# Attention row sums of an adaLN transformer block: transposed and reduced on VectorE in blocks 3 to 14, with a lower threshold for clearing banks on ScalarE

## The chip, the core and the metric

The kernel runs on one core of a Trainium2 chip. The metric is device time in microseconds (us), the median over runs of the same program. The five engines of the core run their own instruction streams in order: TensorE (PE in the profile, its weight loads PEld), VectorE (DVE), ScalarE (ACT), GpSimd (POOL) and SyncE (SP, which issues nearly all transfers here).

## What is computed

One transformer block with adaptive layer norm on 8 sequences of 1024 rows and width 512. The rows are cut in halves of 512, so each sequence gives batches of T = 512, and attention runs over 16 heads of width 32. The reference, cut to what matters:

```python
mod = silu(condition) @ Wada + bada            # six rows of shifts, gains, gates
xm = layernorm(x, g1, be1) * (1 + sc_a) + sh_a
q, k, v = split_heads(xm @ Wqkv)               # 16 heads of width 32
scores = where(causal, q @ k.T * 32 ** -0.5, -inf)
attn = softmax(scores)                         # exp(..) / sum over the keys
x = x + gt_a * (merge_heads(attn @ v) @ Wproj + bproj)
xm = layernorm(x, g2, be2) * (1 + sc_m) + sh_m
x = x + gt_m * (gelu(xm @ W1 + b1) @ W2 + b2)
```

All of it is in float32; the causal mask runs over the full 1024 rows of a sequence. The change concerns the sum over the keys under the softmax, its reciprocal and the division.

## The kernel before, in words

**Blocks.** The work is tiled in 16 blocks n of 512 rows (8 sequences, each with a first half h = 0 and a second half h = 1; odd n are second halves, which look back on the keys of both halves). Each block has four groups g of four heads (HPG = 4; a head has hd = 32 columns, so a group fills the 128 partitions). The dense products (k, q, v, the two layers of the MLP) go through one level of Strassen's scheme with 256-column products; every product is four matmuls side by side, each for 32 of the 128 output partitions (`matmul`, the line 217 of the profile).

**Planner.** The program is built by a Python planner, not by hand. It keeps a clock for each engine (`now`), when each datum is written (`written`) and when its last reader is done (`left`), with estimated costs that `note`, `note_pe` and `note_act` add. A main thread walks through the dense steps of the blocks in the order of `plan`; side threads hold steps that wait for something. The attention (`attend`) is walked in order, and before each of its steps `step_aside` lets dense work go first if that is ready sooner. `stream["due"]` paces the two against each other. So the order of the instructions on each engine comes from the estimates; on the chip each engine simply runs its queue in order.

**Jobs.** Work on VectorE that is not urgent lies in a list (`add_job`); `run_jobs` emits a job when the planner's VectorE is not ahead of TensorE and the job's data are due, `run_jobs(True)` emits all of them at once. Jobs marked `first` go ahead of others.

**Banks.** Three PSUM banks (`banks`, tags l0 to l2) serve all dense products, the row maxima and the row sums. A thread that wants a bank names `BANK` among its needs. They are emptied by `copy_out` (lines 194 and 197, on VectorE or ScalarE, whichever the planner has free sooner) and by `combine_out`, which adds another term: on VectorE straight from the bank (line 208), or, where the planner's VectorE is more than 3500 ns behind its ScalarE, by a copy on ScalarE (line 204) and an addition afterwards on VectorE or GpSimd (`either`, lines 167 and 170). Four more banks hold one tile "st", in turn for scores (line 1595, reduced to maxima on VectorE by lines 1607 and 1610) and for the transposed scores (lines 1674 and 1686, which ScalarE turns into weights by exp, line 1698). One more bank, "po", holds the weighted values of a group (line 1726).

**Weights and slots.** The exponentials of one unit (up to four heads by 512 queries, for 128 keys) lie in a tile `pT` in one of three SBUF slots (`free_p`, tags p0 to p2). The first unit of a group becomes the accumulator `acc`; GpSimd adds the later units of the group onto it (`add_weights`, line 1816). At the end of a group, `finish` has TensorE sum `acc` over the 128 keys that are left: four matmuls by a tile of ones (line 1747), each over 512 columns, into one of the three banks; the result stands in all 32 partitions of its head. Then the slot is free again. ScalarE copies the sums to `rec` (line 1756) and the weighted values to `top` (line 1759); VectorE takes the reciprocals in four jobs of 128 columns (line 1765, `invert`); GpSimd multiplies `top` by `rec` into `qTs[n]` (line 1790, `quotient`), from which the projection `project_out` reads later. With 16 blocks of four groups there are 64 such ends.

Of the kernel before, what the change touches and what calls it, by code (L numbers as in the profile page):

```python
# [9 lines left out]
F32 = mybir.dt.float32  # L10
# [12 lines left out]
def kernel(  # L23
# [89 lines left out]
    def note(engine, ns, reads=(), writes=(), port=False):  # L113
        start = max(now[engine], due(reads, writes))
        if port:
            start = max([start] + [b for a, b in pool_spans if a <= start < b])
        end = start + ns
        now[engine] = end
        if engine == "POOL":
            pool_spans.append((start, end))  # L120
            del pool_spans[:-16]
        for k in reads:
            left[k] = max(left.get(k, 0.0), end + SYNC)
        for k in writes:
            written[k] = end + SYNC
        return end
# [9 lines left out]
    def note_pe(ns, form, reads=(), writes=()):  # L136
        now["PE"] = max(now["PE"], due(reads, writes))
        if shape[0] != form:
            shape[0] = form
            now["PE"] += SWITCH  # L140
        note("PE", ns, reads)
        spent[0] += ns
        for k in writes:
            written[k] = now["PE"] + PIPE

    def note_act(ns, func, reads=(), writes=()):
        if func is not None and table[0] != func:
            table[0] = func
            ns += TABLE
        note("ACT", ns, reads, writes)  # L150
# [49 lines left out]

    def combine_out(out, bank, src, other, reads=(), writes=(), op=ALU.add, last=True):
        ready = due([("l", bank)], writes)
        if op is ALU.add and out is not other and max(now["DVE"], ready) > max(now["ACT"], ready) + 3500:
            nc.scalar.copy(out, src)
            note_act(585, None, [("l", bank)], writes)
            either(out, out, other, op, [*reads, *writes], writes)
        else:
            nc.vector.tensor_tensor(out, src, other, op)  # L208
            note("DVE", 690, [("l", bank), *reads], writes)
        live[bank] = not last  # L210
# [214 lines left out]
    nc.gpsimd.memset(eps, EPS)  # L425
    ones = const.tile([P, hd], F32, tag="ones", name="ones")
    nc.gpsimd.memset(ones, 1.0)
    minus_half = const.tile([P, NTT], F32, tag="minus_half", name="minus_half")
    nc.gpsimd.memset(minus_half, -0.5)
    minus_ones = const.tile([P, P], BF16, tag="minus_ones", name="minus_ones")  # L430
# [122 lines left out]
    def add_job(job, reads, first=False):  # L553

        at = sum(1 for other in jobs if other[2]) if first else len(jobs)
        jobs.insert(at, (job, reads, first))

    def run_jobs(everything=False):
        while jobs and (
            everything or (now["DVE"] <= now["PE"] and due(jobs[0][1]) <= now["PE"])  # L560
        ):
            jobs.pop(0)[0]()
# [841 lines left out]
    def start(it):  # L1404
        thread = [it, None]
        sides.append(thread)
        advance(thread)
# [255 lines left out]
    def weights_T(n, g, parts):  # L1663

        h = blocks[n][1]
        qT = qTs[n]
        reads = [("qT", n), ("kT", n)] + [("mrow", n, gg) for gg in {part[3] for part in parts}]
        step_aside(reads, ["st"])
        st = ps_st.tile([P, HPG, TB], F32, tag="st", name=f"st_{n}_{g}_{parts[0][0]}")
        for k, c0, w, gg in parts:  # L1670
            row = m_rows[n, gg]
            for j in range(HPG):
                r = slice(j * hd, (j + 1) * hd)
                nc.tensor.matmul(  # L1674
                    st[:, j, c0 : c0 + w],
                    minus_ones[r, :],
                    row[r, TB - w :],
                    start=(c0 == 0),
                    stop=False,
                    skip_group_check=True,  # L1680
                )
        for k, c0, w, gg in parts:
            kT = keys_of(n, k // NTT)
            for j in range(HPG):
                r = slice(j * hd, (j + 1) * hd)
                nc.tensor.matmul(  # L1686
                    st[:, j, c0 : c0 + w],
                    kT[r, gg, ts(k % NTT, P)],
                    qT[r, gg, TB - w :],
                    start=False,  # L1690
                    stop=True,
                    skip_group_check=True,
                )
            note_pe(2.5 * COLUMN * w, "rows", reads, ["st"])
        slot = free_p.pop(0)
        pT = pp.tile([P, HPG, TB], F32, tag=f"p{slot}", name=f"pT_{n}_{g}_{parts[0][0]}")
        used = parts[-1][1] + parts[-1][2]
        nc.scalar.activation(pT[:, :, :used], st[:, :, :used], AF.Exp, scale=scale)  # L1698
        note_act(170 + 3.34 * used, "exp", ["st"], [("p", slot)])
        if parts[0][0] >= h * NTT:  # L1700
            for _, c0, _, _ in parts:
                diagonal = pT[:, :, c0 : c0 + P]
                nc.gpsimd.affine_select(  # L1703
                    diagonal,
                    diagonal,
                    pattern=[[0, HPG], [1, P]],
                    compare_op=ALU.is_ge,
                    fill=0.0,
                    base=0,
                    channel_multiplier=-1,  # L1710
                )
                note("POOL", 700, [("p", slot)], [("p", slot)])
        return pT, slot
# [22 lines left out]
    def finish(n, g):  # L1736

        run_jobs(True)
        acc, slot = totals.pop((n, g))
        more = unadded if (n, g) == first_end else []  # L1740
        step_aside([("acc", n, g), *(("p", slot) for *_, slot in more)], [BANK])
        bank = lin_bank()
        terms = [(0, TB, acc, slot)] + [(c0, w, pT, slot) for parts, pT, slot in more for _, c0, w, _ in parts]
        for i, (c0, w, term, held) in enumerate(terms):
            for j in range(HPG):
                r = slice(j * hd, (j + 1) * hd)
                nc.tensor.matmul(  # L1747
                    banks[bank][r, TB - w :], ones, term[:, j, c0 : c0 + w],
                    start=i == 0, stop=i == len(terms) - 1, skip_group_check=True,
                )  # L1750
            note_pe(2 * COLUMN * w, "columns", [("acc", n, g), ("p", held)], [("l", bank)])
        free_p.extend([slot, *(held for *_, held in more)])
        top = tmp.tile([P, TB], F32, tag="top", name=f"top_{n}_{g}", bufs=1)
        rec = tmp.tile([P, TB], F32, tag="rec", name=f"rec_{n}_{g}", bufs=1)
        kr = "rec"
        nc.scalar.copy(rec, banks[bank])  # L1756
        note_act(585, None, [("l", bank)], [kr])
        live[bank] = False
        nc.scalar.copy(top, outs.pop((n, g)))
        note_act(585, None, ["po"], ["top"])  # L1760
        part = TB // 4

        def invert(i):
            some = rec[:, i * part : (i + 1) * part]
            nc.vector.reciprocal(some, some)  # L1765
            note("DVE", 920, [kr], [kr])

        if (n, g) == groups[-1]:
            for i in range(NTT):
                invert(i)  # L1770
                some = slice(i * part, (i + 1) * part)
                nc.vector.tensor_tensor(qTs[n][:, g, some], top[:, some], rec[:, some], ALU.mult)
                note("DVE", 200, [kr, "top"], [("att", n, i)])
            return

        if (n, g) == first_end:
            for i in range(NTT):
                invert(i)
            nc.vector.tensor_tensor(qTs[n][:, g, :], top, rec, ALU.mult)
            note("DVE", 700, [kr, "top"], [("att", n)], port=True)  # L1780
            written["attended", n] = 0.0
            return

        def quotient():
            invert(3)
            if n == NB - 1 and g == NC - 2:
                nc.vector.tensor_tensor(qTs[n][:, g, :], top, rec, ALU.mult)
                note("DVE", 700, [kr, "top"], [("att", n)], port=True)
            else:
                nc.gpsimd.tensor_tensor(qTs[n][:, g, :], top, rec, ALU.mult)  # L1790
                note("POOL", 1285, [kr, "top"], [("att", n)])
            if g == NC - 1:
                written["attended", n] = 0.0

        for i in range(3):
            add_job(lambda i=i: invert(i), [kr], g == NC - 1)
        add_job(quotient, [kr], g == NC - 1)

    shared = {}

# [193 lines left out]
```

## Time and profile before

| | |
|---|---|
| median of 3 runs | 3505.04 us (3502.97 to 3507.28) |
| the profiled execution | 3510.74 us, its span 3509.0 us |
| granted TensorE clock | 0.998 |
| PE, matmuls | 3454.3 us busy |
| DVE | 2198.9 us |
| POOL | 2084.2 us |
| ACT | 1212.4 us |
| first and last row sums of blocks 3 to 14 | 645.5 and 3098.5 us from the span's start |

The profile's rows name a line of the kernel, an engine, the tiles written and read, and how often ("x512"). A float32 matmul is recorded as two instructions, so the four matmuls of one row sum are eight records ("x8"). The row of a timeline has the start, the length, the engine, and in brackets how long the engine had been idle and what ended that. In the view of waits a row has the engine and line that waited, what for, the sum in us, how often, and the longest. In the view of windows a row has the window, its length, and for each engine (in the order PE, PEld, DVE, ACT, POOL, as far as it occurs) the busy us with the count of instructions, then the granted clock, the share of the DMA engines and GB/s.

### The profile page before, as it was taken

How to read it: one execution, taken by the hardware profiler on the slowest of the kernel's cores; microseconds unless marked ns; L12 is line 12 of the kernel's file. 1: busy time of each engine (PE TensorE's matmuls, PEld its weight loads, DVE VectorE, ACT ScalarE, POOL GpSimd, SP SyncE). 2: the span in 40 equal slices, each digit the busy share in tenths (PEclk: the TensorE clock that was granted, in tenths of full speed). 3: DMA queues.
4: the chain of work that ended last, by engine and by line, in shares of the span. 5: the costliest groups of instructions: out<-in, count | busy, mean ns of one | idle time of the engine just before them, and what ended most of it. 6: DMA issues, size and time to landing. Idle time of an engine off the chain costs nothing.

```text
span 3509.0 us, 120365 instructions
## 1 busy us (share of the span) xinstructions
PE 3454.3 (98%) x54429; PEld 1724.0 (49%) x54429; DVE 2198.9 (63%) x2401; ACT 1212.4 (35%) x1276; POOL 2084.2 (59%) x2258
## 2 busy tenths in 40 slices
PE   8999999999999999999999999999999999999999
PEld 4444445445554545445454454544555444554445
DVE  5766676564666656665666566765666756656563
ACT  2335333342233423335223342333423343232531
POOL 3767846666366663756727576275753658537660
PEclk9999999999999999999999999999999999999999
DMA  6843444535545445363454534545354544443334
GB/s 212 263 137 104 137 115 140 142 107 159 142 125 156 119 147 153 119 170 115 137 157 130 155 117 144 150 137 148 116 155 137 165 122 146 128 136 101 96 121 140
DMA packets 328194, 491.10 MB, mean 140 GB/s; under 512 B 27260, under 2 KB 177596, under 8 KB 324100
## 3 DMA queue, kind: packets, MB, share of 16 engines
q1 hardware_dynamic: 327568, 483.39, 47.1%
q8 instruction: 428, 7.01, 0.8%
q14 instruction: 82, 0.67, 0.1%
q10 hardware_dynamic: 116, 0.03, 0.0%
HBM read 425.57 MB, written 55.64 MB: 137 GB/s over the span
## 4 chain that ended last, share of the span: by engine, by line
PE 83%; POOL 7%; DMA 3%; DVE 3%; ACT 1%; issue 1%; SPq 1%; ACTq 0%; DVEq 0%; POOLq 0%
PE bank L217 59%; PE sc L1595 8%; PE st L1686 6%; PE po L1726 6%; POOL pT L1816 4%; PE st L1674 2%; PE bank L1747 2%; DMA hat_m<-held_m 1%; DVE mx L1610 1%; POOL hT L170 1%; ACT pT L1698 1%; DMA held_m<-xm_m 1%; PE bank L1648 0%; POOL xr L170 0%; DMA w<-in_L_cond_Wqkv_dram 0%
## 5 line engine op out<-in xcount | busy, mean ns | idle before, releaser
L1816 POOL TENSOR_TENSOR pT<-pT,pT 128x256 f32<-128x256 f32 (+3 forms) x1254 | 1219.7, 1007 | 298.5 <-PE po L1726 181.6
L1698 ACT ACTIVATE pT<-st 128x2048 f32<-128x2048 f32 x288 | 540.9, 1878 | 1065.1 <-PE st L1686 959.8
L217 PE MATMUL bank<-w,hT 128*32 128x256 f32 x14336 | 823.7, 380 | 0.4 <-issue 0.4
L1610 DVE TENSOR_REDUCE mx<-sc 128x4 f32<-128x2048 f32 (+3 forms) x384 | 665.9, 1755 | 235.6 <-PE sc L1595 229.5
L217 PEld LDWEIGHTS bank<-w,hT 128*32 128x32 f32 x14336 | 446.7, 110 | 390.3 <-issue 105.8
L217 PE MATMUL bank<-xm_m,w 128*32 128x256 f32 x8192 | 498.6, 381 | 3.6 <-ACT xm_m L774 2.2
L217 PE MATMUL bank<-t_m,w 128*32 128x256 f32 x6144 | 382.4, 380 | 0.9 <-DVE t_m L786 0.6
L217 PEld LDWEIGHTS bank<-xm_m,w 128*32 128x32 f32 x8192 | 255.6, 110 | 231.2 <-issue 62.2
L1703 POOL TENSOR_SCALAR_AFFINE_SELECT pT<-pT 128x512 f32<-128x512 f32 x256 | 167.5, 672 | 331.9 <-ACT pT L1698 329.4
L1607 DVE TENSOR_TENSOR sc<-sc,mask 128x1024 f32<-128x1024 f32 (+1 forms) x160 | 162.8, 1018 | 293.3 <-PE sc L1595 237.8
L1595 PE MATMUL sc<-kT,qT 32*128 32x512 f32 (+3 forms) x3072 | 329.5, 521 | 4.3 <-ACT pT L1698 3.3
L1726 PE MATMUL po<-pT,v 128*32 128x512 f32 (+3 forms) x3048 | 301.6, 490 | 3.9 <-POOL pT L1703 3.9
L1686 PE MATMUL st<-qT,kT 32*128 32x512 f32 (+3 forms) x3072 | 300.8, 487 | 0.0
L217 PEld LDWEIGHTS bank<-t_m,w 128*32 128x32 f32 x6144 | 189.6, 110 | 172.9 <-issue 48.5
L1765 DVE RECIPROCAL rec<-rec 128x128 f32<-128x128 f32 x256 | 227.3, 922 | 48.2 <-ACT rec L1756 48.2
L217 PE MATMUL bank<-xm_a,w 128*32 128x256 f32 x3968 | 243.4, 382 | 0.4 <-DMA w<-in_L_cond_Wqkv_dram 0.4
L217 PE MATMUL bank<-w,qT 128*32 128x512 f32 x2048 | 237.0, 595 | 1.1 <-DMA w<-in_L_cond_Wproj_dram 0.7
L1595 PEld LDWEIGHTS sc<-kT,qT 32*128 32x128 f32 x3072 | 129.6, 183 | 188.2 <-issue 88.4
L208 DVE TENSOR_TENSOR hT<-bank,u_u 128x512 f32<-128x512 f32 x187 | 126.6, 686 | 105.8 <-PE bank L217 103.1
L217 PE MATMUL bank<-t_a,w 128*32 128x256 f32 x2944 | 183.2, 380 | 0.0
L217 PEld LDWEIGHTS bank<-xm_a,w 128*32 128x32 f32 x3968 | 123.5, 110 | 110.3 <-issue 29.3
L1115 ACT ACTIVATE hT<-hT,cols 128x512 f32<-128x512 f32 x256 | 164.7, 712 | 35.9 <-DVE hT L208 28.5
(243 smaller groups left out, 3404.0 us busy)
## 6 DMA issues: line engine op xcount, KB each, us to landing
w<-in_L_cond_W_dram SPq DMA_DIRECT2D x384, 256.0 KB
w<-kept_up_S SPq DMA_DIRECT2D x256, 256.0 KB
w<-kept_down_S SPq DMA_DIRECT2D x256, 256.0 KB
w<-kept_qkv_S SPq DMA_DIRECT2D x180, 256.0 KB
w<-in_L_cond_Wqkv_dram SPq DMA_DIRECT2D x147, 256.0 KB
hat_a<-in_x_dram SPq DMA_DIRECT2D x64, 256.0 KB
xr<-in_x_dram SPq DMA_DIRECT2D x32, 512.0 KB
w<-in_L_cond_Wproj_dram SPq DMA_DIRECT2D x64, 256.0 KB
```

Of the source, the lines that this page charges most:

```text
L208: nc.vector.tensor_tensor(out, src, other, op)
L217: nc.tensor.matmul(ps[r, :], columns, rhs, start=start, stop=stop, skip_group_check=True)
L1115: nc.scalar.activation(hT[:, i, :], hT[:, i, :], AF.Gelu, bias=cols[:, O_B1 + f : O_B1 + f + 1])
L1595: nc.tensor.matmul(sc[:, j, c0 : c0 + w], qTs[n][r, gg, ts(qt, P)], keys_of(n, kh)[r, gg, :w], start=True, stop=True, skip_group_check=True,)
L1607: nc.vector.tensor_tensor(place, place, shape_of.to_broadcast(place.shape), ALU.add)
L1610: nc.vector.tensor_reduce(maxima[n, gg][:, kh, qt, :], sc[:, :, c0 : c0 + w], axis=AX.X, op=ALU.max)
L1686: nc.tensor.matmul(st[:, j, c0 : c0 + w], kT[r, gg, ts(k % NTT, P)], qT[r, gg, TB - w :], start=False, stop=True, skip_group_check=True,)
L1698: nc.scalar.activation(pT[:, :, :used], st[:, :, :used], AF.Exp, scale=scale)
L1703: nc.gpsimd.affine_select(diagonal, diagonal, pattern=[[0, HPG], [1, P]], compare_op=ALU.is_ge, fill=0.0, base=0, channel_multiplier=-1,)
L1726: nc.tensor.matmul(po[r, TB - w :], v[:, k % NTT, g * P + j * hd : g * P + (j + 1) * hd], pT[:, j, c0 : c0 + w], start=(k == 0), stop=last ...
L1765: nc.vector.reciprocal(some, some)
L1816: nc.gpsimd.tensor_tensor(into, into, pT[:, j, c0 : c0 + w], ALU.add)
```

## The change

In blocks 3 to 14 (48 of the 64 ends) `finish` hands over to a new function, `finish_turned`. A job on VectorE transposes the whole accumulator in place in squares of 32 by 32 (`turn_acc`: 128 partitions by 2048), so that 32 keys lie along the free axis; a second job sums over them (`sum_acc`: 2048 to 64 values a partition), and only then the slot goes back to `free_p`. What is left are 4 partial sums, one for each group of 32 partitions. A side thread (`spread_sums`) adds these on TensorE: four matmuls by `folded`, four identities of 32 by 32 stacked, of 16 columns each, into a bank. A last job (`invert`) takes the reciprocal of 16 columns out of the bank and spreads it over 512 columns with a second transpose whose input repeats each value 32 times; GpSimd multiplies as before. The copy of the sums on ScalarE goes; that of the values stays, and now comes at once. All three jobs are marked `first`. `weights_T` emits all waiting jobs if no slot is free. `folded` is filled at the start by four copies on GpSimd. In `combine_out`, for all blocks, the threshold falls from 3500 to 500 ns.

```diff
@@ combine_out @@
-        if op is ALU.add and out is not other and max(now["DVE"], ready) > max(now["ACT"], ready) + 3500:
+        if op is ALU.add and out is not other and max(now["DVE"], ready) > max(now["ACT"], ready) + 500:
@@ constants @@
+    folded = const.tile([P, hd], F32, tag="folded", name="folded")
+    for j in range(HPG):
+        nc.gpsimd.tensor_copy(folded[j * hd : (j + 1) * hd, :], ident[j * hd : (j + 1) * hd, j * hd : (j + 1) * hd])
@@ weights_T @@
+        if not free_p:
+            run_jobs(True)
         slot = free_p.pop(0)
@@ finish @@
         acc, slot = totals.pop((n, g))
+        if 2 < n < NB - 1:
+            finish_turned(n, g, acc, slot)
+            return
@@ new @@
+    def finish_turned(n, g, acc, slot):
+
+        top = tmp.tile([P, TB], F32, tag="top", name=f"top_{n}_{g}", bufs=1)
+        rec = tmp.tile([P, TB], F32, tag="rec", name=f"rec_{n}_{g}", bufs=1)
+        nc.scalar.copy(top, outs.pop((n, g)))
+        note_act(585, None, ["po"], ["top"])
+        few = small.tile([P, HPG, HPG * NTT], F32, tag="few", name=f"few_{n}_{g}", bufs=1)
+        inverse = small.tile([P, HPG * NTT], F32, tag="inverse", name=f"inverse_{n}_{g}", bufs=1)
+        turned = acc.rearrange("p j (a i) -> p j a i", i=hd)
+        key = ("few", n, g)
+        written[key] = NEVER
+
+        def turn_acc():
+            flat = acc.rearrange("p j n -> p (j n)")
+            nc.vector.transpose(flat, flat)
+            note("DVE", 2330, [("acc", n, g), ("p", slot)], [("p", slot)])
+
+        def sum_acc():
+            nc.vector.tensor_reduce(few, turned, axis=AX.X, op=ALU.add)
+            note("DVE", 2300, [("p", slot)], [key])
+            free_p.append(slot)
+
+        def spread_sums():
+            yield [key], [BANK]
+            bank = lin_bank()
+            for j in range(HPG):
+                r = slice(j * hd, (j + 1) * hd)
+                nc.tensor.matmul(
+                    banks[bank][r, : HPG * NTT], folded, few[:, j, :],
+                    start=True, stop=True, skip_group_check=True,
+                )
+            note_pe(120, "columns", [key], [("l", bank)])
+
+            def invert():
+                nc.vector.reciprocal(inverse, banks[bank][:, : HPG * NTT])
+                live[bank] = False
+                note("DVE", 260, [("l", bank)], [("inv", n, g)])
+                spread_out = inverse.unsqueeze(2).to_broadcast([P, HPG * NTT, hd])
+                nc.vector.transpose(rec.rearrange("p (a i) -> p a i", i=hd), spread_out)
+                note("DVE", 700, [("inv", n, g)], ["rec"])
+                nc.gpsimd.tensor_tensor(qTs[n][:, g, :], top, rec, ALU.mult)
+                note("POOL", 1285, ["rec", "top"], [("att", n)])
+                if g == NC - 1:
+                    written["attended", n] = 0.0
+
+            add_job(invert, [("l", bank)], True)
+
+        add_job(turn_acc, [("acc", n, g)], True)
+        add_job(sum_acc, [("p", slot)], True)
+        start(spread_sums())
```

## The prediction

> **What bounds the kernel now.** I read the page first: engine shares, then the chain of work that ended last.
>
> ```profile
> span 3509.0 us, 120365 instructions
> PE 3454.3 (98%) x54429; PEld 1724.0 (49%) x54429; DVE 2198.9 (63%) x2401; ACT 1212.4 (35%) x1276; POOL 2084.2 (59%) x2258
> PE 83%; POOL 7%; DMA 3%; DVE 3%; ACT 1%; issue 1%; SPq 1%; ACTq 0%; DVEq 0%; POOLq 0%
> ```
>
> TensorE runs matmuls for 3454.3 of 3509.0 us and holds 83% of the chain. A busy TensorE can hide slow streaming, so the next view is the window in which the 48 changed ends lie, from just before the first to just after the last.
>
> ```profile
> 640.00:3100.00 2460.00, 2444.02 (x38504) 1220.35 (x38499) 1548.96 (x1687) 870.19 (x913) 1484.09 (x1619) 1.00 0.48 138
> ```
>
> There TensorE is without a matmul for 2460.00 - 2444.02 = 16.0 us in all, 0.33 us for each end. VectorE (1548.96, 63%), ScalarE (35%) and GpSimd (60%) have slack on average. So work taken from TensorE should shorten the time one for one, unless what is put elsewhere comes late enough to open gaps. Last, one end in the timeline, the one with the least room behind it that I found (block 5, third group):
>
> ```profile
> 1196.78 0.61 PE L1726 MATMUL po<-pT,v 128*32 128x256 f32 x8
> 1197.21 1.04 PE L1747 MATMUL bank<-pT,ones 128*32 128x512 f32 x8
> 1198.19 0.39 PE L1674 MATMUL st<-mrow,minus_ones 32*128 32x512 bf16 x4
> 1198.40 0.58 ACT L1756 COPY rec<-bank 128x512 f32<-128x512 f32 x1 [0.42 <-PE bank L1747]
> 1199.02 0.95 DVE L1765 RECIPROCAL rec<-rec 128x128 f32<-128x128 f32 x1 [2.16 <-ACT rec L1756]
> 1199.58 1.88 ACT L1698 ACTIVATE pT<-st 128x2048 f32<-128x2048 f32 x1
> 1204.24 1.23 DVE L1607 TENSOR_TENSOR sc<-sc,mask 128x1024 f32<-128x1024 f32 x1 [1.37 <-PE sc L1595]
> 1205.51 2.35 DVE L1610 TENSOR_REDUCE mx<-sc 128x4 f32<-128x1536 f32 x2
> 1212.72 1.04 PE L1726 MATMUL po<-pT,v 128*32 128x512 f32 x8
> ```
>
> The row sums occupy TensorE between two parts of the attention; the slot they free takes an exp 2.4 us after they begin; the matmuls on that exp come at 1212.72.
>
> **The change part by part.** *Removed from TensorE.* The rate first, from the longest unbroken stretch of products, then the count.
>
> ```profile
> 3407.31 97.75 PE bank L217 x1792
> 640.00:3100.00 2460.00, 54.24 (x376) 13.25 (x376) 1.00 0.48 138
> ```
>
> 97.75 us / 1792 = 54.5 ns for a record of 256 columns, four heads side by side; 512 columns are 109 ns, the eight records of an end 0.873 us. The second row (line 1747 alone) has 376 records, 47 of the 48 ends; one end's are missing from the trace. 48 x 0.873 = 41.9 us. The upper bound is the 1.04 us that the example shows from first start to last end, 49.9 us. I take 41.9, since the difference is pipeline fill that its neighbours share.
>
> *Added to TensorE.* Eight records of 16 columns. The trace has none; the nearest rows are matmuls of 8 columns for the modulation, once in a run, once alone.
>
> ```profile
> 132.87 1.14 PE L217 MATMUL bank<-condT,w 128*32 128x8 f32 x104
> 15.05 0.30 PE L217 MATMUL bank<-condT,w 128*32 128x8 f32 x8 [0.35 <-DMA w<-in_L_cond_Wada_dram]
> ```
>
> In the run 1.14 us / 104 = 11.0 ns a record, 0.088 us an end, 4.2 us for 48; alone 0.30 us, 14.4 us. Fitted between products they should be nearer to the run: I take 0.15 us, 7.2 us. [...]
>
> *Waits of TensorE at the sums.* Now the sums wait for GpSimd's additions; after it the few columns wait for VectorE, as the transposed maxima (line 1648) wait for their small operands today.
>
> ```profile
> PEld bank L1747 <- POOL pT L1816: 7.6, 14, 1.4
> PE bank L1747 <- POOL pT L1816: 0.9, 1, 0.9
> PEld L1648 <- POOL mcols L1632: 8.0, 10, 1.7
> PE bank L1648 <- POOL mcols L1632: 3.3, 4, 1.3
> ```
>
> 8.5 us over 64 ends, 6.4 us for 48, go; 11.3 us over 64, 8.5 us for 48, come. I set the pair to zero; the bounds are -6.4 and +8.5.
>
> *VectorE.* Four reciprocals go; a transpose of 2048, a reduction of 2048, a reciprocal of 16 and a transpose of 512 come.
>
> ```profile
> L1765 DVE RECIPROCAL rec<-rec 128x128 f32<-128x128 f32 x256 | 227.3, 922 | 48.2 <-ACT rec L1756 48.2
> 1678.41 2.48 DVE L700 STREAM_TRANSPOSE xm_a<-hat_a 128x512 f32<-128x512 f32 x4
> L1610 DVE TENSOR_REDUCE mx<-sc 128x4 f32<-128x2048 f32 x192 | 439.8, 2291 | 232.3 <-PE sc L1595 229.5
> 11.20 0.18 DVE L636 RECIPROCAL rstd_a<-rstd_a 128x4 f32<-128x4 f32 x1 [0.36 <-ACT rstd_a L634]
> ```
>
> Out: 4 x 0.922 = 3.69 us. In: 2.48 (four transposes of 512 in a row), 2.29, 0.25 (between 0.18 for 4 and 0.922 for 128 columns) and 2.48 / 4 = 0.62: 5.64 us. That is 1.95 us more an end, 94 us in all, and VectorE goes from 63% to some 67% of the window. Covered as a sum, but its form changes: two instructions of 2.3 to 2.5 us stand where four of 0.92 us stood, and whatever is behind them in the queue (bank clearing, masks and maxima) waits. What TensorE pays for each kind today:
>
> ```profile
> PE st L1674 <- DVE mx L1610: 7.8, 8, 2.4
> PEld L1674 <- DVE mx L1610: 28.7, 50, 2.9
> PEld sc L1595 <- DVE mx L1610: 10.1, 20, 1.4
> PEld bank L217 <- DVE rec L1765: 1.1, 2, 0.8
> ```
>
> Behind the maxima, 46.6 us for the 384 reductions of line 1610 (0.12 us each); behind the reciprocals 1.1 us for 256. As the new pair resembles the maxima, I take 96 x 0.12 = 11.6 us of new gaps; the lower bound is 0.4 us (96 at the reciprocals' rate), the upper is the slow rival below.
>
> *The slot.* In the example the exp at 1199.58 uses the slot that the sums freed. Transposing from 1197.4 on, VectorE would free it at 1197.4 + 2.48 + 2.29 = 1202.2 at best, so the exp starts 2.6 us late. What hides it: its reader comes at 1212.72, and dense products fill the time. Without that cover it is 2.6 us at each of the six third groups of odd blocks, 16 us. I take zero.
>
> *ScalarE* loses 48 copies of 0.58 us (28 us), off the path at 35% busy; but the copy of the values no longer stands behind the sums. Zero. *GpSimd* does the same products; its four small copies at the start are hidden in an idle 16.93 us:
>
> ```profile
> 19.55 1.26 POOL L826 TENSOR_TENSOR sums_k<-w,w 128x512 f32<-128x512 f32 x1 [16.93 <-DMA w<-in_L_cond_Wqkv_dram]
> ```
>
> *The threshold.* Combinations on VectorE (line 208) in the window, copies instead on ScalarE (line 204) over the whole span, and the addition that then follows, on GpSimd (170) or VectorE (167):
>
> ```profile
> 640.00:3100.00 2460.00, 341.24 (x499) 1.00 0.48 138
> 0.00:3509.00 3509.00, 11.65 (x20) 1.00 0.48 140
> L170 POOL TENSOR_TENSOR xr<-xr,y 128x512 f32<-128x512 f32 x36 | 46.6, 1299 | 69.2 <-DVE y L208 69.2
> L167 DVE TENSOR_TENSOR xr<-xr,y 128x512 f32<-128x512 f32 x24 | 27.2, 1132 | 1.3
> ```
>
> How many of the 499 move isn't in the trace. If a fifth do, 100 banks are free earlier for a copy of 0.58 us, VectorE is spared 68 us, and 100 additions of 1.1 to 1.3 us come, which fit in GpSimd's idle 976 us. A bank is cleared sooner, its result is ready later; on TensorE I set this to zero, between -12 and +12 us (100 at 0.12 us, either way). [...]
>
> *The sum*, against the profiled execution of 3510.7 us: -41.9 + 7.2 + 0 + 11.6 + 0 + 0 + 0 = -23.1, so 3487.6. That execution was 5.7 us over the median of the runs; against 3505.0 it is **3482 us**. Its own range: at best -41.9 + 4.2 - 6.4 + 0.4 = -43.7, 3461; at worst, with the few columns and the waits at their upper bounds, -41.9 + 14.4 + 8.5 + 11.6 = -7.4, 3498.
>
> **The rivals.**
>
> *Nothing is lost.* The planner covers the new waits, the sums were worth their full 1.04 us: -49.9 + 4.2 - 6.4 = -52, 3453 us. For it: only 16.0 us of gaps in 2460. Against: the transposes make VectorE's pieces longer.
>
> *Given back.* The sums go, but the slots (16 us), the few columns alone (14.4 instead of 7.2) and the threshold's 12 us fall due: all of them give -23.1 + 16 + 7.2 + 12 = +12.1 us, none -23.1; halfway is -5.5, 3500 us. For it: the slot is exposed as soon as VectorE has a mask and maxima in front (1.23 + 2.35 us in the example). Against: dense products lie ready at all times, or the 16.0 us of gaps could not be so few.
>
> *Slower: bank clearing blocked.* Place: the ends at which ScalarE's next instruction is an exp that waits for the slot while VectorE holds mask and maxima (3.6 us) and then transpose and sum (4.8 us). Then neither clears a bank for 8.4 us. A Strassen product of 32 records takes 32 x 54.5 ns = 1.74 us, so three banks last 5.2 us and TensorE stands for 3.2 us. It decides from 35 / 3.2 = 11 such ends on; at half of the 48 it is 77 us against the 41.9 - 7.2 = 34.7 us saved: 3547 us. For it: the jobs are put at the head of the list, and a missing slot emits all at once. Against: the slot is needed at once only at few ends, and the planner knows both durations to within 0.2 us. [...]
>
> *Slower: additions late.* The change of the threshold does not spare VectorE what it says, because the additions come back to it (1.13 us in place of 0.68) or delay GpSimd's sums of weights; 100 of them at 0.6 us exposed: -23 + 60, 3542 us.
>
> **How the numbers follow.** Forecast 0.50; nothing lost 0.12; given back 0.15; banks blocked 0.18; additions late 0.05. A change of 0.2%, 7.0 us, is about what a measurement of this kernel can tell from none: faster is below 3498, slower above 3512. The first two are faster; of "given back" 0.04 is faster, 0.08 the same, 0.03 slower; the last two are slower. Faster 0.66, same 0.08, slower 0.26. The likeliest one's own range is 3461 to 3498. The range for 8 in 10 takes in "nothing lost" and "given back" and the milder part of the blocked banks, up to 17 such ends (-34.7 + 17 x 3.2 = +20): 3452 to 3526.
>
> **What would show it.** Right: TensorE's busy time in the span less by about 35 us, a record of 16 columns near 11 to 20 ns, transpose and sum near 2.4 and 2.3 us, VectorE near 67%, gaps of TensorE in the window below 30 us. Wrong: the reduction or the transpose over 3 us; waits of line 217 for VectorE or ScalarE in tens of us; exps waiting for the reduction for more than some 50 us with TensorE idle beside them. If TensorE's gaps in the window grow past 50 us, the forecast of a gain is wrong.

## The result, and the profile after

The changed kernel takes 3516.67 us (median of 14 runs, 3513.37 to 3521.63), the kernel before 3508.15 us in its 14 runs by then: ratio 1.0024, 95% interval 1.0015 to 1.0032. The forecast was 3482 us; it is slower by some 8 us. The profiled execution took 3514.46 us.

The page after, and the window of the changed ends, which leaves out the last of the 48 (columns as before):

```profile
span 3512.7 us, 120500 instructions
PE 3422.8 (97%) x54429; PEld 1717.4 (49%) x54429; DVE 2330.5 (66%) x2363; ACT 1280.9 (36%) x1402; POOL 2248.6 (64%) x2328
...
640.00:3100.00 2460.00, 2419.00 (x38644) 1215.59 (x38640) 1673.45 (x1669) 911.65 (x991) 1603.06 (x1673) 1.00 0.47 139
```

TensorE is busy for 3454.3 - 3422.8 = 31.5 us less. But the span less TensorE's busy time ("idle" from here on) went from 54.7 to 89.9 us, +35.2, of which 25 lie in the window. And the mean granted clock fell from 0.998 to 0.995, by estimate some 10 us of the span (0.003 x 3512.7), by which matmuls in progress took longer. So about -41.5 us of work, +10 of clock, +35.2 of idle: +3.7 of the span. GpSimd has 164 us more to do, and that is not from the sums, which stay with VectorE and TensorE.

The new instructions, grouped by line with the shapes apart (the last two are one end's columns and the product behind them in the timeline):

```profile
L1821 DVE STREAM_TRANSPOSE pT<-pT 128x2048 f32<-128x2048 f32 x48 | 110.5, 2301 | 5.3 <-POOL pT L1875 5.3
L1825 DVE TENSOR_REDUCE few<-pT 128x64 f32<-128x2048 f32 x48 | 109.4, 2279 | 0.8
L1841 DVE RECIPROCAL inverse<-bank 128x16 f32<-128x16 f32 x48 | 12.0, 250 | 23.6 <-PE bank L1834 23.6
L1845 DVE STREAM_TRANSPOSE rec<-inverse 128x512 f32<-128x512 f32 x48 | 34.1, 711 | 1.8
...
3171.89 0.23 PE L1834 MATMUL bank<-few,folded 128*32 128x16 f32 x8
3171.95 1.05 PE L217 MATMUL bank<-w,hT 128*32 128x256 f32 x16
```

They are what was expected: 2.30 + 2.28 + 0.25 + 0.71 = 5.54 us an end, and the next product starts 0.06 us after the columns. The other edit shows in the windows of four lines over the whole span: 204 (copies on ScalarE in place of a combination), 208 (combinations on VectorE), 170 and 167 (additions on GpSimd and VectorE, those that follow a copy among them):

```profile
0.00:3513.00 3513.00, 128.49 (x222) 0.99 0.47 140
0.00:3513.00 3513.00, 333.85 (x487) 0.99 0.47 140
0.00:3513.00 3513.00, 605.76 (x400) 0.99 0.47 140
0.00:3513.00 3513.00, 374.70 (x328) 0.99 0.47 140
```

The first row had 20 copies and has 222. Line 208 lost 202 combinations and 135.1 us; lines 170 and 167 gained 90 + 112 additions and 118.3 + 114.1 us. So VectorE, which the edit is to spare, is spared 135 - 114 = 21 us, at 232 us of additions on the two engines. One of the new gaps of TensorE, in the timeline:

```profile
1275.08 0.56 ACT L204 COPY y_d<-bank 128x512 f32<-128x512 f32 x1
1275.90 1.91 PE L217 MATMUL bank<-w,t_a 128*32 128x256 f32 x32
1277.06 1.77 POOL L170 TENSOR_TENSOR t_a<-t_a,xm_a 128x512 f32<-128x512 f32 x1 [1.43 <-DVE t_a L789]
1278.79 1.26 POOL L170 TENSOR_TENSOR y_d<-y_d,u_d 128x512 f32<-128x512 f32 x1
1280.08 0.59 ACT L197 COPY p_v<-bank 128x512 f32<-128x512 f32 x1 [4.44 <-POOL y_d L170]
1280.71 1.51 PE L217 MATMUL bank<-w,xm_a 128*32 128x256 f32 x24 [2.90 <-ACT p_v L197]
```

ScalarE copies a bank at 1275.08. The addition that belongs to it stands on GpSimd behind another and ends at 1280.05; until then its operand, a tile with the tag p1, can't be overwritten. The next copy on ScalarE goes into that tile and waits 4.44 us, banks stay full, and TensorE stands for 2.90 us. What follows it is in the windows of that gap and of a stretch 1.4 us after it, and of the largest gap and what follows that:

```profile
1277.80:1280.70 2.90, 0.01 (x2) 0.00 (x0) 0.01 (x1) 0.59 (x1) 2.82 (x3) 1.00 0.52 167
1282.10:1285.50 3.40, 3.40 (x40) 1.69 (x36) 0.00 (x0) 0.59 (x1) 3.40 (x3) 0.50 0.38 91
3175.90:3181.90 6.00, 0.03 (x4) 0.05 (x1) 5.94 (x4) 0.00 (x0) 6.00 (x4) 0.83 0.03 10
3179.90:3186.70 6.80, 4.77 (x24) 1.28 (x27) 1.97 (x1) 1.88 (x1) 2.40 (x3) 0.50 0.01 2
```

The clock (the third column from the right) reads 0.50 in the second and the fourth row: after these gaps the granted clock halves for 3.4 and 6.8 us. So a gap can cost more than its length: from 1280.71 to its next piece of work at 1285.88 TensorE takes 5.17 us for 64 records, which at the 54.5 ns of the prediction are 3.49, so 1.7 us come on top of the 2.90. Not every gap is followed by such a stretch; over the whole span idle time grew by 35.2 us, and the clock took some 10.

The largest gap, 6.00 us, is of another kind. TensorE waits for the row maxima (line 1613, line 1610 before), and these stand on VectorE behind additions:

```profile
3176.37 1.63 DVE L167 TENSOR_TENSOR xr<-xr,v_d 128x512 f32<-128x512 f32 x1
3177.93 1.75 DVE L167 TENSOR_TENSOR xr<-xr,row_gba 128x512 f32<-128x512 f32 x1
3179.60 2.28 DVE L1613 TENSOR_REDUCE mx<-sc 128x4 f32<-128x2048 f32 x1
3181.93 0.61 PE L1677 MATMUL st<-mrow,minus_ones 32*128 32x512 bf16 x4 [6.00 <-DVE mx L1613]
```

TensorE's waits for the maxima came to 7.8 us in the kernel before (shown in the prediction). In the view of waits of the changed one they have grown most, more than those behind copies of ScalarE:

```profile
PE st L1677 <- DVE mx L1613: 20.8, 15, 6.0
PE bank L217 <- ACT p_v L197: 5.4, 2, 2.9
PE bank L217 <- ACT p_k L197: 4.9, 2, 3.2
```

The first row reads 12.1 us in e1 and 11.7 us in e2, the kernels with one of the two edits each (next section). That the additions in front of the maxima lie on VectorE because of the threshold is likely, as line 167 gained 112 of them, but not shown.

### The profile page after: what moved, and what is told of

It reads as the page before. It is cut to its first block, busy times and chain, and to the rows that moved or that the text cites. A ratio compares the mean times of both kernels' runs of the same rounds, so it can differ in the third digit from the quotient of the medians.

```text
span 3512.7 us, 120500 instructions
## 1 busy us (share of the span) xinstructions
PE 3422.8 (97%) x54429; PEld 1717.4 (49%) x54429; DVE 2330.5 (66%) x2363; ACT 1280.9 (36%) x1402; POOL 2248.6 (64%) x2328
## 5 line engine op out<-in xcount | busy, mean ns | idle before, releaser
L1875 POOL TENSOR_TENSOR pT<-pT,pT 128x256 f32<-128x256 f32 (+3 forms) x1254 | 1252.6, 1034 | 205.3 <-ACT pT L1703 117.7
L1708 POOL TENSOR_SCALAR_AFFINE_SELECT pT<-pT 128x512 f32<-128x512 f32 x256 | 177.9, 712 | 228.1 <-ACT pT L1703 226.1
L208 DVE TENSOR_TENSOR hT<-bank,u_u 128x512 f32<-128x512 f32 x134 | 92.3, 690 | 106.8 <-PE bank L217 97.9
L1689 PEld LDWEIGHTS st<-qT,kT 32*128 32x128 f32 x3072 | 143.6, 186 | 26.6 <-issue 1.9
```

The lines of the kernel that those rows point to most:

```text
L1689: nc.tensor.matmul(st[:, j, c0 : c0 + w], kT[r, gg, ts(k % NTT, P)], qT[r, gg, TB - w :], start=False, stop=True, skip_group_check=True,)
L1708: nc.gpsimd.affine_select(diagonal, diagonal, pattern=[[0, HPG], [1, P]], compare_op=ALU.is_ge, fill=0.0, base=0, channel_multiplier=-1,)
L1875: nc.gpsimd.tensor_tensor(into, into, pT[:, j, c0 : c0 + w], ALU.add)
```

## The experiments

Twelve kernels, each against runs of the kernel before on the same chip. "Copies" are those of line 204, "idle" is span less TensorE's busy time, both of the profiled execution.

| kernel | sums | threshold, ns | median, us | ratio (95%) | copies | idle, us | clock |
|---|---|---|---|---|---|---|---|
| before | columns | 3500 | | 1 | 20 | 54.7 | 0.998 |
| the change | turned 3 to 14 | 500 | 3516.67 | 1.0024 (1.0015 to 1.0032) | 222 | 89.9 | 0.995 |
| e1 | turned 3 to 14 | 3500 | 3485.25 | 0.9929 (0.9916 to 0.9941) | 24 | 67.9 | 0.998 |
| e2 | columns | 500 | 3540.84 | 1.0090 (1.0076 to 1.0105) | 198 | 75.6 | 0.995 |
| e3 | 16 columns only | 3500 | 3475.39 | 0.9898 (0.9885 to 0.9912) | 21 | 61.5 | 0.998 |
| e4 | turned 3 to 14 | 1500 | 3520.53 | 1.0025 (1.0014 to 1.0036) | 138 | 96.2 | 0.994 |
| e5 | turned 3 to 14 | never | 3497.12 | 0.9971 (0.9960 to 0.9983) | 0 | 77.5 | 0.996 |
| e6 | turned 1 to 14 | 3500 | 3487.51 | 0.9941 (0.9928 to 0.9955) | 28 | 77.0 | 0.997 |
| e7 | columns | 500, add on VectorE | 3549.73 | 1.0114 (1.0100 to 1.0127) | 191 | 82.6 | 0.995 |
| e8 | columns | 500, add on GpSimd | 3558.52 | 1.0142 (1.0126 to 1.0157) | 199 | 85.0 | 0.995 |
| e9 | columns | 500 if p1 is read | 3517.21 | 1.0024 (1.0015 to 1.0033) | 59 | 56.5 | 0.997 |
| e10 | columns | 500 if p1 is not read | 3535.07 | 1.0072 (1.0060 to 1.0085) | 144 | 68.5 | 0.996 |
| e11 | turned in halves | 3500 | 3488.77 | 0.9947 (0.9935 to 0.9960) | 21 | 68.8 | 0.997 |
| e12 | turned, not first | 3500 | 3495.39 | 0.9958 (0.9946 to 0.9970) | 20 | 77.6 | 0.996 |

The "gaps" in the expectations are counted from the start of the span to the last matmul, some 4 us less than "idle".

**The two edits apart.** e1 is the change with the old threshold, e2 the kernel before with the new one, e4 the change with one between.

```diff
-max(now["DVE"], ready) > max(now["ACT"], ready) + 500     # the change
+max(now["DVE"], ready) > max(now["ACT"], ready) + 3500    # e1; e4: 1500
```

> The change with the threshold left at 3500 ns. Theory T (the lower threshold costs the time: combinations come back later as additions on GpSimd and VectorE, hold their tiles and stall bank clearing): the sums' gain stays, 3508 - 20 to - 40 us, ratio 0.989 to 0.994, TensorE's gaps over the span at most 60 us, hardly any half-speed stretch of the clock between 450 and 3150 us. Rival V (the transposes and reductions on VectorE delay maxima and bank clearing): as slow as the change or slower, ratio 0.998 to 1.006, gaps over 80 us.

> The kernel before with the threshold at 500 ns alone. Theory T: slower than before by 20 to 45 us, ratio 1.006 to 1.013, over 150 copies on ScalarE in combinations, gaps over 85 us. Rival V: no worse than before, ratio 0.997 to 1.003, gaps near 51 us.

> The change with a threshold of 1500 ns. Theory T: between the change and the one with 3500 ns, ratio 0.992 to 0.999, copies on ScalarE in combinations between 20 and 222. Rival V: slower with the higher threshold or no different, ratio 1.001 to 1.006.

e1 gains 0.71%, 25 us; e2 loses 0.90%, 32 us. Together -0.71 + 0.90 = +0.19%, close to the +0.24% of both: they add up. Rival V is out: the same transposes and reductions without the threshold make the kernel faster. T's times came in both; its gaps did not: some 64 us in e1 (at most 60 expected) and 72 us in e2 (over 85 expected). The pages of e1:

```profile
span 3482.3 us, 120253 instructions
PE 3414.4 (98%) x54429; PEld 1711.9 (49%) x54429; DVE 2286.4 (66%) x2403; ACT 1186.8 (34%) x1224; POOL 2086.0 (60%) x2268
```

and of e2:

```profile
span 3541.4 us, 120567 instructions
PE 3465.8 (98%) x54429; PEld 1725.6 (49%) x54429; DVE 2217.3 (63%) x2356; ACT 1297.1 (37%) x1431; POOL 2235.7 (63%) x2335
```

e1: busy 39.9 us less, idle +13.2, clock as before: -26.7 us of span. e2: idle +20.9, and busy +11.5 at a clock of 0.995, which is about the 10 us that 0.3% of the span make: the loss is gaps and what the clock does after them. In e4 the expected half-way point did not come: with 138 copies it is as slow as with 222. The expectation of e4 by T missed; its ratio is in the range of V, which e1 has ruled out. By e1, the 114 copies more cost 0.30 us each there.

**What the columns are worth.** e3 lets TensorE sum only 16 of the 512 columns in blocks 3 to 14.

```diff
-banks[bank][r, TB - w :], ones, term[:, j, c0 : c0 + w],
+banks[bank][r, TB - w : TB - w + min(w, few)], ones, term[:, j, c0 : c0 + min(w, few)],   # few = 16
...
-nc.scalar.copy(rec, banks[bank])
+some = banks[bank][:, :few].unsqueeze(2).to_broadcast([P, few, TB // few])   # each column 32 times
+nc.scalar.copy(rec.rearrange("p (a i) -> p a i", a=few), some)
```

> The kernel before, but in blocks 3 to 14 the sums run over the first 16 of 512 columns, and ScalarE spreads these 16 (the other columns' sums are left out); VectorE, slots and threshold as before. What the columns of TensorE are worth by themselves. Both theories: 48 x (0.87 - 0.1) = 37 us less, ratio 0.988 to 0.991, gaps near 51 us. If under 20 us are gained, the columns were not worth their length on the path, and the gain was never there.

36 us, near the 37 expected: most of the length of the removed columns was on the path. TensorE is busy for 45.5 us less (3408.8 us) and idle for 6.8 us more. e1 keeps 25 of the 36.

**Why a moved combination costs.** e7 and e8 fix the engine of the addition; e9 and e10 split the combinations by whether they read p1, the tile of the gap shown above.

```diff
-either(out, out, other, op, [*reads, *writes], writes)
+nc.vector.tensor_tensor(out, out, other, op)              # e7; e8: nc.gpsimd; each with its estimate
...
-max(now["DVE"], ready) > max(now["ACT"], ready) + 500
+max(now["DVE"], ready) > max(now["ACT"], ready) + (500 if "p1" in reads else 3500)   # e9; e10 the other way
```

> The kernel before with the threshold at 500 ns, the addition after a copy always on VectorE. Theory G (the cost comes from GpSimd: its queue is long, the additions behind it come late and push its sums of weights back): most of the 32 us go, ratio 0.998 to 1.004, GpSimd busy near 2084 us. Theory L (any addition after a copy comes late, whichever engine does it, since VectorE was late when the copy was chosen): still 1.006 or more.

> The same with the addition always on GpSimd. Theory G: worse than with the choice, ratio 1.010 to 1.020, GpSimd busy over 2280 us. Theory L: near the choice, 1.006 to 1.011.

> The kernel before with 500 ns only for combinations that read the tile p1 (there is one; the first copy of each Strassen product or of a step down takes it next), 3500 ns for all others. Theory H (the late addition holds p1, the next copy into p1 waits on ScalarE, and TensorE runs out of banks): most of the 32 us, ratio 1.005 to 1.010, waits of line 197 for line 170 or 167 in the list of waits. Theory N (each moved combination costs alike, 32 us / 178 = 0.18 us): about a third of the moved ones read p1, so ratio 1.002 to 1.004.

> The complement: 500 ns for combinations that do not read p1, 3500 ns for those that do. Theory H: ratio 0.998 to 1.003. Theory N: ratio 1.005 to 1.008.

Theory H, my reading of the first gap above as the main cause, fell, and N came out in both. In e9 the 59 - 20 = 39 additional copies that hold p1 cost 0.24%, 8 us, 0.22 us each; in e10 124 others cost 0.72%, 25 us, 0.20 us each. So p1 is not what makes a copy dear. G and L are both half right. With all additions on VectorE the cost is 40 us for 171 copies, 0.23 us each, so it is not GpSimd's queue alone; with all on GpSimd it is 50 us for 179, 0.28 us each, within what G expected. The planner's choice between the two (e2, 32 us for 178, 0.18 us each) is the best of the three, and still a loss.

How late the results come can be read from the traces, if each copy of line 204 is paired with the next addition into the same tile. From the start of the copy to the end of its addition it takes 2.45 us in the change, 2.74 us in e2, 2.79 us in e7, 4.21 us in e8 (medians), where a combination of line 208 takes 0.69 us. That is more than the bare 0.58 + 1.1 to 1.3 us, as the addition waits in a queue, and e8, with the latest results, is the dearest. It fits a price set by the delay.

A rival remains that no run separates. Every edit here also changes the planner's clocks, and with them the order of what follows. In e2 about two thirds of TensorE's pieces of work (matmuls in a row of one line and the same tiles) stand in the same order as before; the rest is another schedule. For the delay: e9 keeps over nine tenths of the order, and its copies cost 0.22 us each all the same. Against a fixed price per copy: e4 and the change share nine tenths of theirs, and 138 or 222 copies make no difference. So 0.16 to 0.30 us a copy is an average over the schedules tried, and how much of it is delay and how much another order is open.

e5 asks about the few copies that 3500 ns leaves.

```diff
-max(now["DVE"], ready) > max(now["ACT"], ready) + 500
+max(now["DVE"], ready) > max(now["ACT"], ready) + 1e9
```

> The change with the copy on ScalarE never taken in a combination (the 24 that remain at 3500 ns go too). If each moved combination costs some 0.2 us whatever VectorE's lateness, 24 x 0.2 = 5 us better than with 3500 ns: ratio 0.991 to 0.993. If the few that 3500 ns still moves are those where VectorE is really late, worse than with 3500 ns: ratio 0.994 or more.

Without any copy the kernel is slower than with 24 (0.9971 against 0.9929, the intervals apart), idle 77.5 against 67.9 us. The second expectation came: the few that are left at 3500 ns pay, some 15 us for 24. Of the four settings tried with the turned sums (500, 1500, 3500, never) 3500 ns is the best. One reading is that a copy pays only where VectorE is late by more than the copy delays the result. Paired as above, the results take 3.14 us in e4 and 4.45 us in e1 in place of 0.69: a delay well over 1500 ns in e4, and of about 3500 ns in e1. No run tests this by itself.

**What the turned sums cost themselves.** e1 has 13.2 us of idle time that the kernel before hasn't. e11 cuts transpose and reduction in two, e12 puts the jobs behind others, e6 turns blocks 1 and 2 as well.

```diff
-add_job(turn_acc, [("acc", n, g)], True)
+for i in range(2):                                        # e11, sum_acc likewise
+    add_job(lambda i=i: turn_acc(i), [("acc", n, g)], True)
...
+add_job(turn_acc, [("acc", n, g)], g == NC - 1)           # e12, all three jobs
...
-if 2 < n < NB - 1:
+if 0 < n < NB - 1:                                        # e6
```

> The change in blocks 3 to 14 with 3500 ns, transpose and reduction each in two halves as jobs of their own (1024 elements, some 1.2 us). If the 13 us of gaps that the turned sums added come from the length of the two instructions: gaps fall from 64 towards 51 us, ratio 0.988 to 0.991. If they come from the work as such, or from its place ahead of other jobs: gaps over 60 us, ratio 0.992 to 0.995 (some 0.1 us an end more on VectorE).

> The change in blocks 3 to 14 with 3500 ns, its three jobs placed behind other jobs as the reciprocals were before (first only in the last group of a block). If the 13 us of gaps come from the place ahead of maxima and normalization: gaps fall to 51 to 57 us, ratio 0.988 to 0.991, faster than any run so far that computes all of it. If they come from VectorE's added work or from slots that come free later: gaps 60 us or more, exps waiting longer for the reduction than 65 us, ratio 0.992 to 0.996.

> The change in blocks 1 to 14 (56 ends) with 3500 ns. If each end is worth what it was in blocks 3 to 14 (25.8 us / 48 = 0.54 us): 30 us, ratio 0.990 to 0.993. If blocks 1 and 2, where weights are still being prepared, have no room on VectorE: ratio 0.993 to 0.997.

Halves leave the idle time where it was (68.8 against 67.9 us). That does not clear the length of the instructions: in the trace of e11, 20 times in 48 ends all four halves still run back to back on VectorE, 4.8 us on end. Behind other jobs it is worse, 77.6 us, and the waits show one reason. From the view of waits of e1:

```profile
ACT pT L1703 <- DVE few L1825: 65.0, 11, 13.0
```

and of e12:

```profile
ACT pT L1703 <- DVE few L1825: 111.5, 14, 16.2
```

The exps wait longer for the slot. So the place at the head of the list is right. The slot may be part of the price; how the 13.2 us divide between slots and the 87.5 us that VectorE has more to do in e1 is open. Blocks 1 and 2 bring nothing: e6 is not faster than e1. No run beat e1 while computing all of it.

## Why the prediction was wrong

The measured 3516.67 us lies inside the range for 8 in 10 (3452 to 3526), but that is luck: its upper end was worked out for blocked banks, and something else happened.

*What bounds the kernel* held: TensorE's columns were worth their time (e3, 36 us; forecast 41.9 - 7.2 = 34.7). That a busy TensorE can hide slow streaming shows in the changed kernel: from 1282.10 it is busy for all 3.40 us, at a clock of 0.50.

*Removed and added on TensorE* held. In e1, at the same mean clock, TensorE's busy time falls by 39.9 us, in e3 by 45.5 us; forecast 34.7. That the difference between 41.9 and 49.9 us is pipeline fill was the author's estimate; from the start of the sums to that of the next matmuls it is 0.97 us at 39 ends of the kernel before and 0.86 at 15. The few columns were taken too dear: from their start to that of the next product it is 0.06 or 0.08 us at most ends, as in the rows at 3171.89, against the 0.15 taken, and near the row's 0.088. One reading was wrong: no end is missing from the trace. The last changed end starts at 3171.98 us, behind the window, where line 1747 has the records of five ends and block 15 has only four:

```profile
3100.00:3509.00 409.00, 7.03 (x40) 1.63 (x40) 0.99 0.40 119
```

*VectorE* held: 5.54 us an end (forecast 5.64). *New gaps* from its two long instructions were forecast as 11.6 us; e1 shows 13.2 us. That the size was right is luck. Of the 46.6 us taken as TensorE's price for the maxima, 38.8 are waits of weight loads (PEld), which overlap matmuls (1724.0 us beside 3454.3 us of matmuls in a span of 3509.0); TensorE itself waited for 7.8 in these rows, and in the whole window it was without a matmul for 16.0 us. And whether the length of the instructions makes the gaps is open after e11: to break them up in halves brought nothing there (idle 68.8 against 67.9 us).

*The slot* was set to zero with a bound of 16 us. Exps do wait for the reduction, 65 us in e1, but ScalarE has room (34% busy there). With longer waits in e12 TensorE's idle time grows too; that the one causes the other is not shown. Waits of more than some 50 us had been named, with TensorE idle beside them, as a sign of being wrong; e1 has them and is faster than the kernel before.

*The sum of all of these* was -23.1 us. e1, which is just these, measures -25 us.

*The threshold* is the step that failed. It was set "to zero, between -12 and +12 us (100 at 0.12 us, either way)". It costs 33 us on top of the turned sums (1.0024 against 0.9929) and 32 us alone. Three things were off. The count: 146 more copies in the window (158 by the row of line 204 there, less 12), and edits outside of blocks 3 to 14 too, 202 in all. The price: 0.16 to 0.30 us a copy where 0.12 was taken from the maxima. And the sign: a bank cleared earlier was to make up for a result that comes later. The rows for that stood in the prediction, 0.58 us of copy and 1.1 to 1.3 us of addition for 341.24 / 499 = 0.68 us; it asks whether GpSimd has the time, not who waits for the result. VectorE behind ScalarE by half a microsecond is less than the 1.0 to 1.2 us that the detour of copy and addition takes longer by these rows, and in the traces it takes 1.8 us longer (2.45 against 0.69). That the threshold costs this time is shown by e1 and e2; that it does so by late results is seen in single gaps and fits the runs, beside the rival of the changed order.

*The rivals.* "Additions late" was this mechanism and had a chance of 0.05 and a price of 3542 us, worked out for 100 additions at 0.6 us; measured were twice as many at 0.16. "Banks blocked" had 0.18; e1 shows that the turned sums as such do not cost the gain. The sentence that gaps past 50 us in the window would speak against a gain was too lax: 41 were enough, since 10 of the 35.2 us of new idle time lie outside the window, and the clock comes on top.

*Clock.* Not in the sum at all: by the profiles of the change and of e1, TensorE is idle for 22.0 us more and, at the lower clock, busy for 8.4 us more with the same matmuls, so a quarter of the loss.

## What to carry to other kernels

A change of two parts is two sums: the part that looked like an aside cost more than the main one gained. Clearing a PSUM bank by a copy and adding later replaces one pass by two, and by these runs it paid only where the engine that would do it in one pass was taken to be some microseconds late (3500 ns, against 500 and 1500). Price the moved count from the rows of both forms, with the queue in which the addition waits, and ask who waits for the later result. When a planner makes the order, a changed threshold is a changed schedule as well. Where TensorE is busy all the time, count with each new gap the stretch at half clock that may follow it (here 3.4 us after 2.90 us without matmuls).

## What the runs showed of the hardware

- In the changed kernel the granted clock halves for 3.4 us or 6.8 us after gaps that are shorter than that: after 2.90 us without matmuls from 1277.8, it is 0.50 from 1282.1 to 1285.5; after 6.00 us from 3175.9, from 3179.9 to 3186.7.
- Eight float32 records of 16 columns, in four column groups, cost TensorE little between products: at most ends of the change and of e1 the next product starts 0.06 or 0.08 us after them, 8 to 10 ns a record.
- A transpose on VectorE in squares of 32 takes 2301 ns for 2048 float32 columns in place, and 711 ns for 512 columns that are read from 16 values each repeated 32 times; an input with repeated values costs little over a plain one of 512 columns (674 ns on average, line 703).
- Which gaps are followed by half clock can be read from the traces. In the trace of the kernel before and in that of the changed one the stretches at half clock start whole multiples of 3.4133 us apart, to within 0.01 us (the changed kernel's at 145.43, 394.60, 438.98, 1282.07, 1992.04, 3179.88, 3405.16 and 3510.97); this is the grid below. A gap of 2.42 us at 1988.7 lies in one window of the grid, and the next window is at half clock (the first two rows, from the changed kernel). A longer gap of 3.20 us at 1092.6 is split between two windows, with 1.80 and 1.41 us idle, and none follows (the other three):

```profile
1988.64:1992.05 3.41, 0.99 (x16) 0.41 (x12) 2.29 (x1) 0.89 (x2) 3.41 (x5) 1.00 0.79 182
1992.05:1995.46 3.41, 3.41 (x32) 1.38 (x32) 2.18 (x3) 3.41 (x4) 3.41 (x6) 0.50 0.02 5
1090.93:1094.35 3.42, 1.62 (x32) 0.71 (x24) 0.00 (x0) 0.00 (x0) 3.42 (x4) 1.00 0.19 66
1094.35:1097.76 3.41, 2.00 (x40) 1.20 (x40) 1.99 (x4) 2.37 (x3) 3.25 (x3) 1.00 0.09 31
1097.76:1101.17 3.41, 3.41 (x56) 1.59 (x52) 1.98 (x3) 1.06 (x2) 3.41 (x4) 1.00 0.65 216
```

In these two traces, from 40 us on and without the last window with matmuls, six windows of the grid had 2.24 to 3.41 us idle, and each was followed by one at half clock. Six had 1.85 to 2.06 us: five were followed by one, that at 924.16 in the kernel before (1.89 us) was not.
